# Some of the listed products of a graph layer, computed from 12-bit parts instead of in plain fp32

## The chip, the cores and the metric

The kernel runs on one core of one Trainium2 chip. The metric is the device time of one execution in microseconds; a comparison takes several runs of both kernels on the same chip. The profile is one further execution, recorded by the hardware profiler.

## The reference

Four layers work on a feature matrix x of 2708 x 512 and one sparse, symmetric-patterned adjacency matrix adj of 2708 x 2708. Each layer normalises its input, takes the relu, and adds its result to x. The layer that the change touches is layer 2:

```python
def _L2_gnn_ref(x, adj, W1, b1, W3, b3, Wf, bf):
    h = jax.nn.relu(adj @ (x @ W1) + b1)
    h = jax.nn.relu(adj @ (h @ W3) + b3)
    return jnp.tanh(h @ Wf + bf)
...
h = jnp.maximum(_layernorm(x, axis=-1), 0.0)
x = x + _L2_gnn_ref(h, adj, L2_gnn_W1, L2_gnn_b1, L2_gnn_W3, L2_gnn_b3, L2_gnn_Wf, L2_gnn_bf)
```

Everything is fp32. The adjacency matrix is dense in its first columns and rows and sparse in the rest: the chance of an entry falls with the square root of the row's and the column's number.

## The kernel before, in words

**Tiles.** The 2708 nodes are 22 row tiles of 128 (the last has 20). For a row tile m, the product adj @ g is made of two kinds of products of 128 x 128 by 128 x 512. The first six column tiles (DENSE = 6) are taken whole. Of the others, only the columns that hold an entry in this row tile are taken: layer 0 makes a list of them (`make_lists`, L290), and gathers and stores the adjacency columns that belong to the list (`listed`). `CHUNKS` (L38) tells how many products of 128 listed columns a row tile needs: none for tile 0, 10, 9 and 8 for tiles 1 to 3, 7 for tiles 4 to 7, then 6 and 5, and 2 for tile 21. That is 130 in all. Tile 0 has no list and takes all its column tiles (the `else` branch at L873); tile 21 has no dense part.

**Dense products in parts.** A dense piece of the adjacency (three tiles, 128 x 384) is loaded as `raw` and split into a 12-bit high part `hi`, the rest `lo`, and a sum `s` (L850 on ScalarE, L851 and L852 on VectorE). The features g are split likewise (`split_b`, L177). Three products in the type fp32r, hi x hi and lo x lo into the bank `main` and s x s into the bank `mixed`, take the place of one fp32 product (L863); the factors that `sum_banks` (L738) and the scales apply make the sum right. The buffers a_hi, a_lo and a_s have two copies each.

**Listed products.** `gather` (L810, issued at L814 on POOL) fetches for each product 128 rows of g from DRAM into one of eight buffers gg0 to gg7, which are used in turn over all row tiles. `load_listed` (L805) brings the adjacency columns as `ac`. Each listed product is one plain fp32 matmul into `mixed` (L866), in the order of the list, and is the last work of a row tile. `main` ends with the last dense product.

**The passes.** Layer 2 has two passes over the row tiles. The first (L956, order 0 to 9, 21, 10 to 20) aggregates g1 = h @ W1, adds the bias, takes relu, splits (`relu_parts`, L750) and multiplies by W3 (`project3`, L768: twelve fp32r products), and stores g2. While it works on tile 0 it also makes g1. It also writes a uint8 mask of the nonzero entries (L832) for layer 3. The second pass (L1125, order 0, 6 to 9, 21, 10 to 20, 1 to 5) aggregates g2, multiplies by Wf, applies tanh, adds to x, normalises, and multiplies by the weights of layer 3.

**Buffers of weights.** `wr` (1 MB, one buffer) is where a weight matrix lands before `split_w` splits it. In the first pass it holds Wf, which is split once tile 0 is done, and then the weights of layer 3, w_d, are loaded into it at once (L961). They are split into wb0 to wb2 in the second pass at tile 0 (L1129). Later `room` (L1005) hands out `wr` first as four places for gathers of layer 3, the first of which are issued with the last tile of the second pass.

**The order of the work.** The program is written as a sequence, and a scheduler fixes the order of each engine's instructions when the kernel is built: among those that its timing model takes to be ready, the one that comes first in the program goes first, and a buffer is given out when a previous user has released it. On the chip each engine runs its instructions in that fixed order; the DMA queues of SP and POOL too. So the dense products of row tile m+1 appear between the listed products of tile m and its projection. All of it lies in one function, of which the parts named here are the inner functions.

Of the kernel before, what the change touches and what calls it, by code (L numbers as in the profile page):

```python
# [8 lines left out]
FP = mybir.dt.float32  # L9
FR = mybir.dt.float32r  # L10
# [5 lines left out]
AF = mybir.ActivationFunctionType  # L16
ALU = mybir.AluOpType
# [4 lines left out]
P = 128  # L22
# [19 lines left out]
def kernel(  # L42
# [47 lines left out]
    def dense_of(m):  # L90

        return 0 if m == NT - 1 else DENSE
# [726 lines left out]
            )  # L819
        return gs  # L820

    def aggregate(m, parts, shifted, gd, marked):


        n = rows(m)
        whole, num = dense_of(m), CHUNKS[m]
        if marked:
            nz = ap.tile([P, NMARK, P], U8, name="nz", bufs=3)

            def mark(i, a):  # L830
                k, ts = a.shape[:2]
                nc.scalar.activation(nz[:k, i : i + ts, :n], a, AF.Sign)  # L832
        main = ps_a.tile([P, D], FP, name="agg") if dense_of(m) else None
        mixed = ps_a.tile([P, D], FP, name="aggs")
        chunks = []
        if num:
            ac = load_listed(m)
            chunks = [(ac[:, c, :], g) for c, g in enumerate(gather(m, gd))]
            if marked:
                mark(whole, ac)  # L840
        for ts in dense if dense_of(m) else []:
            gs = [parts(t) for t in ts]
            raw, k = load_piece(m, ts)
            hi, lo, s = (
                ap.tile([P, PIECE, P], FR, name=f"a_{part}") for part in ("hi", "lo", "s")
            )
            d = (slice(0, k), slice(0, len(ts)), slice(0, n))
            if marked:
                mark(ts[0], raw)
            nc.scalar.activation(hi[d], raw, AF.Copy, scale=UP)  # L850
            nc.vector.tensor_tensor(lo[d], raw, hi[d].bitcast(FP), ALU.subtract)  # L851
            nc.vector.scalar_tensor_tensor(  # L852
                s[d], lo[d].bitcast(FP), SHIFT, hi[d].bitcast(FP), op0=ALU.mult, op1=ALU.add
            )
            for i, t in enumerate(ts):
                ghi, glo, gs_ = gs[i]
                first, last = t == 0, t == DENSE - 1
                for acc, a, b, st, sp in (
                    (main, hi, ghi, first, False),
                    (main, lo, glo, False, last),  # L860
                    (mixed, s, gs_, first, False),
                ):
                    nc.tensor.matmul(acc[:n], a[:k, i, :n], b[:k], start=st, stop=sp)  # L863
        if chunks:
            for c, (a, g) in enumerate(chunks):
                nc.tensor.matmul(  # L866
                    mixed[:n],
                    a,
                    g,
                    start=(c == 0 and not dense_of(m)),  # L870
                    stop=(c == len(chunks) - 1),
                )
# [12 lines left out]
    def aggregated(m, parts, shifted, gd, bias, marked=False):  # L885
        n = rows(m)
        u = wp.tile([P, D], FP, name="u")
        main, mixed = aggregate(m, parts, shifted, gd, marked)
# [78 lines left out]
    bf = load_bias(bf_d, "bias0")  # L967
    bl = load_bias(b_d, "bias2")

# [659 lines left out]
```

## Time and profile before

| | us |
|---|---|
| median of 3 runs | 1551.56 |
| lowest and highest run | 1547.21, 1553.23 |
| the profiled execution | 1471.58 |
| its span, first to last instruction | 1469.7 |
| layers 0 and 1, and tile 0 of the first pass, in the span | 0 to about 641 |
| first pass of layer 2, tiles 1 to 20 | about 641 to 907 |
| seam: tile 0 of the second pass | about 907 to 945 |
| second pass of layer 2, other tiles | about 945 to 1262 |
| layer 3, the rest | about 1262 to 1470 |

The profiled execution has its own time, below the median of the unprofiled runs; durations are taken from it.

How to read the profile: PE is TensorE's matmul, PEld its weight load, DVE VectorE, ACT ScalarE, POOL GpSimd; SPq is the queue of SyncE, which issues most DMAs. A group's row gives the line, engine and operation, the tiles written and read, the count, then the busy time in us and the mean of one in ns, then the engine's idle time just before it and who ended it. A plain fp32 product has two MATMUL records, an fp32r product one. Matmuls are pipelined, so their cost is read from the distance of their starts and not from their length. In a stretch, each engine has its busy time and, in brackets, its instructions; then come the granted TensorE clock, the mean busy share of the 16 DMA engines, and the data rate. In the timeline the columns are start, length, engine, line, operation, tiles, count, and in square brackets the idle time before it and what ended it.

### The profile page before, as it was taken

The numbers are of one execution on the slowest core, as the hardware profiler recorded it, in microseconds if no ns is written. First come the engines' busy times: TensorE is split into PE (matmuls) and PEld (weight loads), VectorE is DVE, ScalarE is ACT, GpSimd is POOL, SyncE is SP. The second block draws the span as 40 slices with busy tenths as digits, with TensorE's granted clock in tenths as the row PEclk, the third lists the DMA queues.
The fourth block names the chain that finished last, engine by engine and source line by source line (L and its number), as shares of the span: only waits on it lengthen the run. The fifth ranks groups of instructions, "written<-read, shape, count | busy, mean of one in ns | idle before, by whom it ended". The sixth has DMA issues, their size and how long they took to land. (4 is left out here: it accounts for less than half of the span.)

```text
span 1469.7 us, 15561 instructions
## 1 busy us (share of the span) xinstructions
PE 1343.2 (91%) x4474; PEld 767.6 (52%) x4474; DVE 960.7 (65%) x1876; ACT 736.5 (50%) x1152; POOL 691.2 (47%) x690
## 2 busy tenths in 40 slices
PE   5489989999999869989999999899999999868997
PEld 2123334434334346755655666466677666656665
DVE  2566998998999679643433447365666665656675
ACT  5987864965521256432333335244554545454453
POOL 1162465876784341055554441333433445247763
PEclk9699989999999979999999999999999999889999
DMA  8896677788866398377786777856555666478884
GB/s 300 301 324 206 220 269 252 242 283 298 296 224 212 105 362 269 105 233 251 251 245 213 230 235 223 263 163 198 160 187 163 191 202 216 134 242 255 255 278 158
DMA packets 182415, 338.58 MB, mean 230 GB/s; under 512 B 25727, under 2 KB 94251, under 8 KB 178589
## 3 DMA queue, kind: packets, MB, share of 16 engines
q1 hardware_dynamic: 134929, 188.00, 38.1%
q0 software_dynamic: 47392, 149.51, 32.8%
q8 instruction: 37, 0.61, 0.2%
q14 instruction: 57, 0.47, 0.1%
HBM read 276.34 MB, written 61.09 MB: 230 GB/s over the span
## 5 line engine op out<-in xcount | busy, mean ns | idle before, releaser
L866 PE MATMUL aggs<-gg,ac 128*128 128x512 f32 (+1 forms) x520 | 232.7, 594 | 3.4 <-DMA gg<-g1d,idx_g 3.3
L814 POOL DMA_INDIRECT gg<-g2d,idx_g x130 | 131.2, 1009 | 217.6 <-PE aggs L866 168.6
L814 POOL DMA_INDIRECT gg<-g1d,idx_g x130 | 133.6, 1028 | 171.8 <-PE aggs L866 101.6
L478 POOL DMA_INDIRECT ac<-in_adj_t_dram,idx_a x130 | 144.8, 1114 | 79.8 <-issue 34.8
L660 PE MATMUL acc<-h,inc 128*128 128x512 f32 (+1 forms) x348 | 171.6, 626 | 6.4 <-ACT h L168 3.5
L496 POOL DMA_INDIRECT h<-h0d,idx_g x111 | 117.3, 1057 | 84.1 <-PE acc L660 58.8
L866 PEld LDWEIGHTS aggs<-gg,ac 128*128 128x128 f32 (+1 forms) x520 | 97.3, 188 | 110.6 <-issue 101.2
L850 ACT ACTIVATE a_hi<-raw 128x384 fp32r<-128x384 f32 x84 | 43.5, 520 | 158.0 <-issue 87.0
L863 PE MATMUL agg<-ghi,a_hi 128*128 128x512 f32 x252 | 115.0, 456 | 3.0 <-ACT a_hi L850 2.8
L660 PEld LDWEIGHTS acc<-h,inc 128*128 128x128 f32 (+1 forms) x348 | 63.8, 197 | 83.1 <-issue 65.6
L660 PE MATMUL acc<-h,incl 128*128 128x512 f32 (+1 forms) x222 | 104.3, 608 | 0.0
L863 PE MATMUL agg<-glo,a_lo 128*128 128x512 f32 x252 | 102.1, 405 | 1.3 <-ACT glo L189 1.3
L814 POOL DMA_INDIRECT gg<-hidr,idx_h x79 | 80.0, 1012 | 45.4 <-issue 13.1
L863 PE MATMUL aggs<-gs,a_s 128*128 128x512 f32 x252 | 100.2, 400 | 0.7 <-DVE a_s L852 0.6
L851 DVE TENSOR_TENSOR a_lo<-raw,a_hi 128x384 fp32r<-128x384 f32 x84 | 47.2, 562 | 76.4 <-ACT a_hi L850 49.9
L146 PE MATMUL yacc<-wvo,hT 128*128 128x512 f32 (+1 forms) x176 | 88.5, 642 | 4.2 <-ACT hT L175 4.2
L760 DVE SCALAR_TENSOR_TENSOR v_lo<-pt,v_hi 128x512 fp32r<-128x512 f32 (+1 forms) x88 | 56.5, 664 | 45.5 <-ACT v_hi L759 45.2
L741 DVE SCALAR_TENSOR_TENSOR u<-aggs,u 128x512 f32<-128x512 f32 x42 | 28.9, 687 | 75.4 <-PE aggs L866 73.9
L759 ACT ACTIVATE v_hi<-pt 128x512 fp32r<-128x512 f32 (+1 forms) x88 | 48.7, 579 | 44.1 <-PE pt L754 41.9
L660 PEld LDWEIGHTS acc<-h,incl 128*128 128x128 f32 (+1 forms) x222 | 40.7, 190 | 52.4 <-issue 50.8
L429 ACT ACTIVATE sgn<-ar 128x2708 bf16<-128x2708 f32 (+1 forms) x22 | 54.0, 2457 | 26.1 <-DMA ar<-in_adj_dram 22.5
L460 DVE FIND_INDEX8 at_top<-top,ar 128x8 uint32<-128x2708 f32 (+1 forms) x22 | 65.3, 2970 | 0.0
(268 smaller groups left out, 2897.1 us busy)
## 6 DMA issues: line engine op xcount, KB each, us to landing
ar<-in_adj_dram SPq DMA_DIRECT2D x27, 1354.0 KB
raw<-in_adj_t_dram SPq DMA_DIRECT2D x108, 192.0 KB
slot<-x SPq DMA_DIRECT2D x41, 256.0 KB
at<-in_adj_t_dram SPq DMA_DIRECT2D x27, 384.0 KB
ac<-lst SPq DMA_DIRECT2D x16, 384.0 KB
h<-in_x_dram SPq DMA_DIRECT2D x21, 256.0 KB
h0d<-h POOLq DMA_DIRECT2D x21, 256.0 KB, 5.7
xt<-in_x_dram SPq DMA_DIRECT2D x21, 256.0 KB
```

What stands on the lines that cost most here:

```text
L146: nc.tensor.matmul(acc[:n], hT[:, c, :n], w[:, c, :], start=(c == 0), stop=(c == NCD - 1))
L429: nc.scalar.activation(sgn[:n], ar[:n], AF.Sign, accum_out=sum_sgn[:n])
L460: nc.vector.max_index(at_top[:n], top[:n], ar[:n])
L478: nc.gpsimd.indirect_dma_start(out=ac[:, c, :n], out_offset=None, in_=adj_units, in_offset=bass.IndirectOffsetOnAxis(ap=idx_a[:, m, c0 + c ...
L496: nc.gpsimd.indirect_dma_start(out=g, out_offset=None, in_=h0d[:, :], in_offset=bass.IndirectOffsetOnAxis(ap=idx_g[:, m, c : c + 1], axis=0),)
L660: nc.tensor.matmul(acc[:n], a, g, start=(i == 0), stop=(i == len(pairs) - 1))
L759: nc.scalar.activation(hi[d], pt[d], AF.Relu, scale=UP)
L760: nc.vector.scalar_tensor_tensor(lo[d], pt[d], 0.0, hi[d].bitcast(FP), op0=ALU.max, op1=ALU.subtract)
L814: nc.gpsimd.indirect_dma_start(out=gs[c], out_offset=None, in_=gd[:, :], in_offset=bass.IndirectOffsetOnAxis(ap=index[:, m, c : c + 1], ax ...
L851: nc.vector.tensor_tensor(lo[d], raw, hi[d].bitcast(FP), ALU.subtract)
L863: nc.tensor.matmul(acc[:n], a[:k, i, :n], b[:k], start=st, stop=sp)
L866: nc.tensor.matmul(mixed[:n], a, g, start=(c == 0 and not dense_of(m)), stop=(c == len(chunks) - 1),)
```

## The change

In row tiles that have both a dense part and a list, the first `in_parts` listed products are computed from parts: three in the first pass, two in the second, and none in the last two row tiles of the second pass (tiles 4 and 5). Tiles 0 and 21 stay as they are. The other listed products stay plain fp32 and come first; the products in parts come last and end both banks. For them the adjacency columns in `ac` are split by ScalarE and VectorE like a dense piece, in one operation for all two or three, with the low part then rescaled on ScalarE. Each gathered row block is split by one ScalarE and two VectorE operations; its low part takes the place of the gathered rows, and its high part and sum go into one of two pairs of slots in the buffer `wr`. So w_d is no longer loaded early in the first pass but after it, and `wr` is used as slots again in the second pass once w_d has been split.

```diff
+    def split_a(raw, k, ts, n, scale_lo=None):
+        hi, lo, s = (
+            ap.tile([P, PIECE, P], FR, name=f"a_{part}") for part in ("hi", "lo", "s")
+        )
+        d = (slice(0, k), slice(0, ts), slice(0, n))
+        nc.scalar.activation(hi[d], raw, AF.Copy, scale=UP)
+        nc.vector.tensor_tensor(lo[d], raw, hi[d].bitcast(FP), ALU.subtract)
+        nc.vector.scalar_tensor_tensor(
+            s[d], lo[d].bitcast(FP), SHIFT, hi[d].bitcast(FP), op0=ALU.mult, op1=ALU.add
+        )
+        if scale_lo:
+            nc.scalar.activation(lo[d], lo[d].bitcast(FP), AF.Copy, scale=scale_lo)
+        return hi, lo, s
+
+    row_slot, part_rows = [0], [None]
+
+    def split_row(g):
+        i = row_slot[0] % 2 * 2
+        row_slot[0] += 1
+        hi, s = part_rows[0][:, i, :], part_rows[0][:, i + 1, :]
+        lo = g.bitcast(FR)
+        nc.scalar.activation(hi, g, AF.Copy, scale=UP * EPS12)
+        nc.vector.scalar_tensor_tensor(
+            lo, g, EPS12, hi.bitcast(FP), op0=ALU.mult, op1=ALU.subtract
+        )
+        nc.vector.scalar_tensor_tensor(
+            s, lo.bitcast(FP), SHIFT, hi.bitcast(FP), op0=ALU.mult, op1=ALU.add
+        )
+        return hi, lo, s
...
+        in_parts = in_parts if whole and num else 0
...
-                first, last = t == 0, t == DENSE - 1
+                first, last = t == 0, t == DENSE - 1 and not in_parts
...
-            for c, (a, g) in enumerate(chunks):
+            for c, (a, g) in list(enumerate(chunks))[in_parts:]:
                 nc.tensor.matmul(
                     mixed[:n],
                     a,
                     g,
-                    start=(c == 0 and not dense_of(m)),
-                    stop=(c == len(chunks) - 1),
+                    start=(c == 0 and not whole),
+                    stop=(c == num - 1 and not in_parts),
                 )
+            if in_parts:
+                hi, lo, s = split_a(ac[:, :in_parts], P, in_parts, n, -SHIFT)
+                for c in range(in_parts):
+                    ghi, glo, gs_ = split_row(chunks[c][1])
+                    last = c == in_parts - 1
+                    for acc, a, b, sp in (
+                        (main, hi, ghi, False),
+                        (main, lo, glo, last),
+                        (mixed, s, gs_, last),
+                    ):
+                        nc.tensor.matmul(acc[:n], a[:, c, :n], b, start=False, stop=sp)
...
     for m in order_m:
         n = rows(m)
-        parts = aggregated(m, first_parts, first_product, g1d, bias1, marked=True)
+        parts = aggregated(m, first_parts, first_product, g1d, bias1, True, 3)
         if m == 0:
             wf = split_w(wset, wr, "wa")
-            wr = load_w(wset, w_d, "wr")
+            part_rows[0] = wset.tile([P, NCD, D], FR, name="wr")
...
+    wr = load_w(wset, w_d, "wr")
     bf = load_bias(bf_d, "bias0")
...
     for m in order_2:
         n = rows(m)
-        parts = aggregated(m, second_parts, second_product, g2d, bias3)
+        in_parts = 0 if m in order_2[-2:] else 2
+        parts = aggregated(m, second_parts, second_product, g2d, bias3, False, in_parts)
         if m == 0:
             w = split_w(wsetb, wr, "wb")
+            part_rows[0] = wset.tile([P, NCD, D], FR, name="wr")
```

More of the change, by code (lines that the diff above doesn't have):

```diff
@@ L820, in gather, with aggregate @@
         return gs
-    def aggregate(m, parts, shifted, gd, marked):
+    def split_a(raw, k, ts, n, scale_lo=None):
[25 more added lines that the diff above has]
+        return hi, lo, s
+    def aggregate(m, parts, shifted, gd, marked, in_parts):
         n = rows(m)
         whole, num = dense_of(m), CHUNKS[m]
+        in_parts = in_parts if whole and num else 0
         if marked:
@@ L843, in aggregate @@
             raw, k = load_piece(m, ts)
[L844 to L847, printed above, removed]
             if marked:
                 mark(ts[0], raw)
[L850 to L854, printed above, removed]
+            hi, lo, s = split_a(raw, k, len(ts), n)
             for i, t in enumerate(ts):
                 ghi, glo, gs_ = gs[i]
-                first, last = t == 0, t == DENSE - 1
+                first, last = t == 0, t == DENSE - 1 and not in_parts
                 for acc, a, b, st, sp in (
@@ L883, in aggregate, with aggregated @@
         return main, mixed
-    def aggregated(m, parts, shifted, gd, bias, marked=False):
+    def aggregated(m, parts, shifted, gd, bias, marked, in_parts):
         n = rows(m)
         u = wp.tile([P, D], FP, name="u")
-        main, mixed = aggregate(m, parts, shifted, gd, marked)
+        main, mixed = aggregate(m, parts, shifted, gd, marked, in_parts)
         if dense_of(m):
```

## The prediction

> **What bounds the kernel now.** I read the busy shares first, then the costliest groups, then stretches of the span by stage, then one row tile of the first pass in order of time, then the gathers' time to landing. The page and its groups:
>
> ```profile
> PE 1343.2 (91%) x4474; PEld 767.6 (52%) x4474; DVE 960.7 (65%) x1876; ACT 736.5 (50%) x1152; POOL 691.2 (47%) x690
> ...
> L866 PE MATMUL aggs<-gg,ac 128*128 128x512 f32 (+1 forms) x520 | 232.7, 594 | 3.4 <-DMA gg<-g1d,idx_g 3.3
> L814 POOL DMA_INDIRECT gg<-g1d,idx_g x130 | 133.6, 1028 | 171.8 <-PE aggs L866 101.6
> ...
> L863 PE MATMUL agg<-ghi,a_hi 128*128 128x512 f32 x252 | 115.0, 456 | 3.0 <-ACT a_hi L850 2.8
> ```
>
> L866 is the listed products: 520 records for 260 products (130 a pass), so a product has two records. TensorE waits 3.4 us for all of them; the gathers' idle time (L814) is spent waiting for L866 to free a buffer. By stage (the two passes over the row tiles, and the seam between them):
>
> ```profile
> core 0: us, PE busy (x) PEld busy (x) DVE busy (x) ACT busy (x) POOL busy (x), PEclk, DMA share, GB/s
> 641.00:907.00 266.00, 262.88 (x924) 160.95 (x925) 112.44 (x187) 87.44 (x162) 126.82 (x126) 0.99 0.76 242
> 945.00:1262.00 317.00, 315.46 (x1206) 209.19 (x1205) 199.71 (x373) 156.85 (x234) 130.37 (x130) 1.00 0.60 185
> ...
> 907.00:945.00 38.00, 31.89 (x103) 19.07 (x102) 15.82 (x28) 10.09 (x19) 8.04 (x8) 0.91 0.79 259
> ```
>
> In both passes TensorE is busy 99% of the time at full clock; VectorE 42% and 63%, ScalarE 33% and 49%. Time taken off TensorE there is time off the kernel, as long as the others keep up. One tile of seven products in the first pass, in order of time:
>
> ```profile
> 703.36 0.39 PE L863 MATMUL aggs<-gs,a_s 128*128 128x512 f32 x1
> 703.59 6.17 PE L866 MATMUL aggs<-gg,ac 128*128 128x512 f32 x14
> ...
> 704.88 1.18 POOL L814 DMA_INDIRECT gg<-g1d,idx_g  x1 [3.15 <-PE aggs L866]
> 706.37 0.95 POOL L814 DMA_INDIRECT gg<-g1d,idx_g  x1 [0.30 <-PE aggs L866]
> 707.62 0.94 POOL L814 DMA_INDIRECT gg<-g1d,idx_g  x1 [0.30 <-issue]
> ...
> 709.82 0.39 PE L863 MATMUL agg<-glo,a_lo 128*128 128x512 f32 x1
> 709.87 0.69 DVE L741 SCALAR_TENSOR_TENSOR u<-aggs,u 128x512 f32<-128x512 f32 x1 [3.96 <-PE aggs L866]
> ...
> 711.43 0.63 PE L754 MATMUL pt<-ident,u 128*128 128x128 f32 x4
> ...
> 717.29 6.17 PE L866 MATMUL aggs<-gg,ac 128*128 128x512 f32 x14
> ```
>
> The period is 13.70 us (703.59 to 717.29). Fourteen records and one L863 lie between 703.59 and 709.82: (6.23 - 0.23) / 7 = 0.857 us a listed product. The dense part products (L863) start 0.23 us apart (703.36, 703.59), so three cost 0.69 us. While u (L741, L891) is summed, TensorE takes seven of the next tile's dense products: this is its cover. The gathers follow the freed buffers at 1.25 us each, the first 1.29 us after the block begins. Their landing, in the middle of the pass:
>
> ```profile
> DMA to landing us min/median/max: 3.5/4.5/5.8
> ```
>
> [...]
>
> **The change part by part.** *Products.* First pass: 20 tiles (all but 0 and 21) x 3 = 60; second: 20 less the last two = 18 tiles x 2 = 36. Each turns 0.857 into 0.69 us, 0.167 less: 60 x 0.167 = 10.0 and 36 x 0.167 = 6.0, together -16.0 us on TensorE, which sets the end of both passes.
>
> *Splits of the adjacency pieces.* Per tile two ScalarE and two VectorE operations. First pass at 384 columns: L850 0.52, L851 and L852 0.56 each. [...]
>
> *Splits of the gathered rows.* Each product adds L179's shape on ScalarE (0.62) and L183's and L186's on VectorE (0.69 + 0.68). So VectorE gets, per tile, 1.12 + 3 x 1.37 = 5.2 us in the first pass (20 x: 105) and 0.85 + 2 x 1.37 = 3.6 in the second (18 x: 65). Its share becomes (112 + 105) / 256 = 85% and (200 + 65) / 311 = 85%. ScalarE gets 1.04 + 1.86 = 2.9 (58 in all) and 0.84 + 1.24 = 2.1 (37): (87 + 58) / 256 = 57% and (157 + 37) / 311 = 62%. All of it lies beside TensorE's 256 and 311 us; I take 0. If that cover fails at the end of each tile, the cost is the slower rival's.
>
> *The end of a tile.* main now stops with the last split product, so the sum starts with ScalarE's 0.58 (L740) after it, which was long done before. Also c2, the third split row, waits for the pair of hi and s that c0 used: hi 0.62, lo 0.69, s 0.68, about 2.4 with handovers, against c1's 0.69 of products. What is late next is the sum of u; the cover is the next tile's 18 dense products, 18 x 0.23 = 4.1 us. I take 0. What is queued behind the waiting row split on VectorE and ScalarE is the next tile's a_lo and a_hi, for which TensorE would wait. Bounds: 0 to 2 us a tile; not below zero, since nothing leaves this chain.
>
> *Gather buffers.* There are eight, taken in turn, and the first of a tile's buffers is the one that POOL needs first, but it is now used last. In a tile of seven, four plain products (3.4) and hi and lo of c0 (0.46) come before it is free: with the 0.43 that the trace shows after a product's end, the first gather goes at 4.3 instead of 1.3. One buffer was spare, six follow: the last goes at 4.3 + 5 x 1.25 = 10.6 and lands at 15.1. It is needed at (13.70 - 0.50) + 3 x 0.857 = 15.8: on time by 0.7 us at the median landing, late by 0.6 at the longest. Tiles of six and five have two and three spare buffers, so are safe. Wider ones are not. Tile 2 (nine, behind ten) starts at buffer 2, tile 1's c2, free at about 6.0 + 2.0 + 0.4 = 8.4; its nine gathers land by 8.4 + 8 x 1.25 + 4.5 = 22.9, needed at about 15.5 + 5 x 0.857 = 19.8. Three late; as the scheduler can put the split products (2.1) first, 1 to 3, I take 2. Tile 3 likewise: 6.7 + 8.75 + 4.5 = 20.0 against 18.4, late by 1.6, I take 1; tile 4, whose first buffer isn't spare either, 0.5. Tile 1 itself: TensorE already waits 3.3 us for the first row (at 641.27), which must now be split (2 us) or passed over: +1, bounds -2 (see the moved load) to +3. Second pass: more work lies between two blocks (period 16.0), only tile 1 (ten) and tile 2 refill from themselves: +1, bounds 0 to 4.
>
> *The moved load.* The 1 MB load of wr (L152) leaves 634.6, where the queues are at 90 to 100% and the first gather is late, for the end of the pass, when c2 of the last tile frees the buffer, about 908 on SP. There bias loads, x2, raw and listed pieces queue behind it, and POOL's gathers share the engines. From 910 to 920 the DMA share is 0.31 and 0.79, so 4.5 us of all engines are free for about 3 us of data at the 340 to 390 GB/s of 920 to 935. But right after, TensorE waits 5.4 us for raw pieces: I take +1, bounds -1 to +4. The weights' own splits have until 952.
>
> Sum: -16.0 + 3.5 (tiles 2 to 4) + 1 + 1 + 1 = -9.5 us. The profiled execution takes 1471.6 (span 1469.7), so 1462; the median of the three runs, 1551.6, is 80 us above it, which the profile doesn't explain, so I carry the difference over: 1551.6 - 9.5 = 1542.
>
> **The rivals.**
> *Full gain.* The scheduler orders around the late gathers and the freed 1 MB helps tile 1: -16, 1536. For it: TensorE had almost no waits before. Against: the buffer count above.
> *Late gathers throughout.* The tiles of seven slip too (0.6 and more, twelve wide tiles over both passes)[...]: 12 x 0.7 = 8 more, 1550, no change.
> *VectorE sets the second pass.* 85% in an order fixed in advance, with tanh and the normalisation between: the second pass gains nothing (6 back) and loses 0.1 us a tile: 1550.
> *The end of a tile is exposed* (slower). The split piece takes one of the two a_ buffers, so the next tile's second half of dense products (9 x 0.23 = 2.1) can't be split before the last listed product. Chain from c0's products to the transposes: 0.62 + 0.69 + 0.68 + 0.58 + 0.69 + 0.69 plus seven handovers of 0.15 = 5.0 us; cover without that half is 0.69 + 2.1 = 2.8. Up to 2.2 are bare; half of it on 20 tiles is +22: 1542 + 22 = 1564. It decides from 9.5 / 20 = 0.5 us a tile. Against it: the two parts of the chain overlap with the dense products' own splits (1.9 us).
> That the change does nothing is excluded: the products exist in every tile.
>
> **How the numbers follow.** Forecast 46% (of it 6% within the bound), full gain 14%, late gathers 12%, VectorE 8%, exposed end 20%. 0.5%, about what a measurement of this kernel can tell from no change, is 7.8 us. Faster: 0.40 + 0.14 = 0.54; same: 0.06 + 0.12 + 0.08 = 0.26; slower 0.20. Half the exposed cases end below 1564, so the range is 1532 to 1564, with some 15% outside. The likeliest side's own range is 1532 to 1543.
>
> **What would show it.** Right: L866 falls from 520 to 328 records; split products 0.23 us apart; TensorE still 98 to 99% busy in both passes; periods of seven near 13.2 and second-pass periods of six near 15.7; short waits of L866 for gg in tiles 1 to 4 only; VectorE near 85%. Wrong: a TensorE wait of over 0.5 us in each tile, on a row split, on a_hi or on u; waits for gg in tiles of seven or six; or a seam longer by more than 4 us.

## The result, and the profile after

The changed kernel takes 1655.91 us (median of 3 runs, 1643.7 to 1657.72) against 1551.56: 1.0656 times the time before, 95% interval 1.057 to 1.0742. It is slower, and outside the range that was given. Its profiled execution has a span of 1654.1 us. The page (busy row, then groups):

```profile
PE 1403.1 (85%) x4570; PEld 814.6 (49%) x4570; DVE 1105.8 (67%) x2144; ACT 822.1 (50%) x1324; POOL 703.0 (42%) x690
...
L814 POOL DMA_INDIRECT gg<-g1d,idx_g x130 | 137.3, 1056 | 227.1 <-PE aggs L893 132.5
L893 PE MATMUL aggs<-gg,ac 128*128 128x512 f32 (+1 forms) x328 | 164.6, 626 | 35.8 <-DMA gg<-g1d,idx_g 25.0
```

L866 is L893 now: 328 records, as forecast. But TensorE waits 35.8 us for gathered rows in front of them, where it waited 3.4. The first pass, the second pass and the seam between them:

```profile
core 0: us, PE busy (x) PEld busy (x) DVE busy (x) ACT busy (x) POOL busy (x), PEclk, DMA share, GB/s
688.00:1016.00 328.00, 285.50 (x999) 185.30 (x998) 203.59 (x347) 139.28 (x259) 128.68 (x124) 0.92 0.63 197
1045.00:1405.00 360.00, 323.82 (x1224) 218.58 (x1223) 244.21 (x464) 180.01 (x294) 135.08 (x127) 0.96 0.52 160
1016.00:1045.00 29.00, 22.74 (x59) 11.38 (x58) 13.54 (x23) 9.00 (x16) 8.84 (x8) 0.89 0.93 307
```

The profile of the kernel before that the prediction read is 80 us under that kernel's median, and the two traces differ in layers 0 and 1 too, which the change doesn't touch. So I took one more profiled execution of the kernel before (e1), whose span is 1536.8. Its two passes:

```profile
680.00:962.00 282.00, 273.40 (x958) 168.15 (x959) 117.54 (x195) 91.87 (x170) 126.59 (x126) 0.99 0.73 233
990.00:1313.00 323.00, 320.44 (x1222) 212.18 (x1221) 202.26 (x378) 158.57 (x236) 131.18 (x130) 1.00 0.60 184
```

The first pass is 46 us longer (328 against 282): 34 us more in which TensorE is idle (42.5 against 8.6), and 12 us more in which it is busy, at a clock of 0.92 in place of 0.99. The second is 37 us longer in these stretches, 34 of them idle. The stretches were cut by eye and the changed kernel's end earlier in the work, the second by about one row tile; between the same points of the work (the table below) the passes are 54 and 59 us longer. The loss lies in the two passes, in TensorE's waits and in the lower clock beside them (0.92 for 0.99 and 0.96 for 1.00).

One tile of the changed kernel's first pass, in order of time (weight loads, VectorE and most products left out):

```profile
801.15 0.84 ACT L867 ACTIVATE nz<-ac 128x768 uint8<-128x768 f32 x1 [2.25 <-DMA ac<-lst]
...
801.44 0.95 POOL L814 DMA_INDIRECT gg<-g1d,idx_g  x1 [0.30 <-issue]
...
801.75 0.60 PE L754 MATMUL pt<-ident,u 128*128 128x128 f32 x4
801.90 0.51 ACT L828 ACTIVATE a_hi<-ac 128x384 fp32r<-128x384 f32 x1
...
802.88 0.40 PE L890 MATMUL aggs<-gs,a_s 128*128 128x512 f32 x1
...
803.74 0.63 ACT L846 ACTIVATE wr<-gg 128x512 fp32r<-128x512 f32 x1 [1.33 <-DMA gg<-g1d,idx_g]
804.28 0.51 ACT L867 ACTIVATE nz<-raw 128x384 uint8<-128x384 f32 x1
...
804.69 0.58 ACT L759 ACTIVATE v_hi<-pt 128x512 fp32r<-128x512 f32 x1
...
805.94 1.66 PE L893 MATMUL aggs<-gg,ac 128*128 128x512 f32 x2 [2.67 <-DMA gg<-g1d,idx_g]
...
806.61 2.70 PE L779 MATMUL main<-wb,v_hi 128*128 128x512 f32 x4
...
809.10 1.42 PE L779 MATMUL main<-wb,v_lo 128*128 128x512 f32 x4
```

The transposes (L754) are done at about 802.3, and v_hi (L759), which the projection (L779) needs, could follow at once. Ahead of it in ScalarE's fixed order stand four things of the next tile: the mark of its listed columns (L867, it waits 2.25 us for the load of `ac`), the high part of the columns of three products (L828), a row split (L846, waits 1.33 us for a gathered row) and a mark of a dense piece. The first two are through at 802.4; in this tile it is the row split's wait that holds v_hi back, until 805.27. Ahead of the projection in TensorE's order stands a plain listed product of the next tile (L893); its row was issued at 801.44 and is there at 805.94, 4.5 us later and 0.67 us after v_hi, so here that is the wait that ends last. TensorE idles 2.67 us, and then two groups of four projection products take 2.70 us (with the end of the plain product in it) and 1.42 us, where the kernel before needs about 1.1. There, in e1, the order is the other way round:

```profile
772.61 0.60 ACT L759 ACTIVATE v_hi<-pt 128x512 fp32r<-128x512 f32 x1
...
773.34 1.12 PE L779 MATMUL main<-wb,v_hi 128*128 128x512 f32 x4
...
774.56 0.85 ACT L832 ACTIVATE nz<-ac 128x768 uint8<-128x768 f32 x1 [1.34 <-DMA ac<-lst]
```

From row tile 3 on, the mark of `ac` follows v_hi of the tile before in every row tile of the kernel before, and stands ahead of it in every one of the changed kernel but tile 11. TensorE's order changed too: in the changed kernel's first pass a plain listed product of the next tile stands between the transposes and the projection in 12 row tiles, and TensorE waits for its row 9 times, 17.4 us in all; in the kernel before this is so in none. TensorE's two largest waits in the changed kernel's first pass, 688 to 1016 (engine, line, the one waited for, us in total, times, longest; the first also holds 7.6 us in tiles 1 and 2, at the listed products' own place):

```profile
PE aggs L893 <- DMA gg<-g1d,idx_g: 25.0, 12, 4.2
PE main L779 <- ACT v_hi L759: 11.3, 6, 4.1
```

The second pass has no marks. A tile of it in the changed kernel, in order of time:

```profile
1116.99 1.03 PE L754 MATMUL pt<-ident,u 128*128 128x128 f32 x8
...
1118.34 0.39 PE L890 MATMUL aggs<-gs,a_s 128*128 128x512 f32 x1
...
1122.26 1.29 ACT L846 ACTIVATE wr<-gg 128x512 fp32r<-128x512 f32 x2 [5.22 <-DMA gg<-g2d,idx_g]
...
1123.45 1.07 ACT L759 ACTIVATE v_hi<-pt 128x512 fp32r<-128x512 f32 x2
...
1124.09 2.07 PE L779 MATMUL main<-wb,v_hi 128*128 128x512 f32 x4 [5.36 <-ACT v_hi L759]
...
1125.96 1.05 PE L779 MATMUL main<-wb,v_lo 128*128 128x512 f32 x2
```

Two row splits wait 5.22 us for gathered rows, two v_hi are queued behind them, and TensorE waits 5.36 us for the first of them; then it works at half speed for some 3 us (the granted clock is 0.50 from 1123.84 to 1127.25).

### The profile page after: what moved, and what is told of

It is laid out like the page before. It is cut to its first block, busy times and chain, and to the rows that moved or that the text cites. A ratio compares the mean times of both kernels' runs of the same rounds, so it can differ in the third digit from the quotient of the medians.

```text
span 1654.1 us, 16430 instructions
## 1 busy us (share of the span) xinstructions
PE 1403.1 (85%) x4570; PEld 814.6 (49%) x4570; DVE 1105.8 (67%) x2144; ACT 822.1 (50%) x1324; POOL 703.0 (42%) x690
## 5 line engine op out<-in xcount | busy, mean ns | idle before, releaser
L893 PE MATMUL aggs<-gg,ac 128*128 128x512 f32 (+1 forms) x328 | 164.6, 626 | 35.8 <-DMA gg<-g1d,idx_g 25.0
L660 PE MATMUL acc<-h,inc 128*128 128x512 f32 (+1 forms) x348 | 172.8, 630 | 3.7 <-ACT h L168 1.2
L146 PE MATMUL yacc<-wvo,hT 128*128 128x512 f32 (+1 forms) x176 | 100.1, 714 | 25.3 <-issue 13.3
L847 DVE SCALAR_TENSOR_TENSOR gg<-gg,wr 128x512 fp32r<-128x512 f32 x96 | 65.4, 687 | 72.5 <-ACT wr L846 54.7
L846 ACT ACTIVATE wr<-gg 128x512 fp32r<-128x512 f32 x96 | 59.6, 626 | 101.2 <-PE agg L910 28.4
L890 PE MATMUL agg<-ghi,a_hi 128*128 128x512 f32 x252 | 103.2, 410 | 5.5 <-ACT a_hi L828 4.2
L893 PEld LDWEIGHTS aggs<-gg,ac 128*128 128x128 f32 (+1 forms) x328 | 61.7, 196 | 91.3 <-issue 40.3
L660 PE MATMUL acc<-h,incl 128*128 128x512 f32 (+1 forms) x222 | 104.7, 611 | 0.0
L660 PEld LDWEIGHTS acc<-h,inc 128*128 128x128 f32 (+1 forms) x348 | 64.6, 199 | 80.6 <-issue 70.7
L779 PE MATMUL main<-wb,v_hi 128*128 128x512 f32 (+1 forms) x176 | 67.1, 511 | 24.0 <-ACT v_hi L759 22.5
L850 DVE SCALAR_TENSOR_TENSOR wr<-gg,wr 128x512 fp32r<-128x512 f32 x96 | 65.4, 684 | 15.8 <-PE aggs L910 14.5
L146 PEld LDWEIGHTS yacc<-wvo,hT 128*128 128x128 f32 (+1 forms) x176 | 36.8, 221 | 75.1 <-issue 57.8
L830 DVE SCALAR_TENSOR_TENSOR a_s<-a_lo,a_hi 128x384 fp32r<-128x384 f32 (+1 forms) x122 | 64.9, 534 | 9.9 <-PE aggs L910 2.7
L759 ACT ACTIVATE v_hi<-pt 128x512 fp32r<-128x512 f32 (+1 forms) x88 | 48.4, 575 | 44.4 <-PE pt L754 32.0
```

Source lines behind the costliest of these rows:

```text
L146: nc.tensor.matmul(acc[:n], hT[:, c, :n], w[:, c, :], start=(c == 0), stop=(c == NCD - 1))
L660: nc.tensor.matmul(acc[:n], a, g, start=(i == 0), stop=(i == len(pairs) - 1))
L779: nc.tensor.matmul(acc[:n], a[:, c, :n], b[:, c, :], start=first and c == 0, stop=last and c == NCD - 1,)
L830: nc.vector.scalar_tensor_tensor(s[d], lo[d].bitcast(FP), SHIFT, hi[d].bitcast(FP), op0=ALU.mult, op1=ALU.add)
L847: nc.vector.scalar_tensor_tensor(lo, g, EPS12, hi.bitcast(FP), op0=ALU.mult, op1=ALU.subtract)
L850: nc.vector.scalar_tensor_tensor(s, lo.bitcast(FP), SHIFT, hi.bitcast(FP), op0=ALU.mult, op1=ALU.add)
```

## The experiments

**Theories.** Q: the row splits and the re-ordered plain products wait for gathered rows and stand, in an order fixed at build time, ahead of the previous tile's v_hi and projection. M, formed after e8: in the first pass the marks do the same, waiting for the loads of the adjacency. W: the splits' work on ScalarE and VectorE is itself the bound. B: the split of the listed adjacency holds one of the two a_ buffers. L: late gather buffers in tiles of seven and more. (That the order is kept on the chip is seen where both programs are still the same: the first 1593 matmul records of TensorE, 564 instructions of ScalarE, 1052 of VectorE, 562 of GpSimd and 279 DMA issues of SyncE come in the same sequence in the profiles of before and after, though the second is 43 us behind at the first product in parts.)

**How they are read.** Ratios are to the kernel before on the same chip. The runs were made in batches, each on another chip: e1 to e4 on chip 0, e5 to e7 on chip 1, e8 to e10 on chip 6, e11 to e14 on chip 5, e15 to e17 on chip 8, e18 on chip 7; for the result and the first profile no chip is recorded. The stages come from each profiled execution: first pass from the end of layer 1's products (L660) to the last store of g2, second pass from there to the last store of the tiles' results `hid`. Where the kernel before takes about 1480 us, layers 0 and 1 take 499 to 509 us, and where it takes about 1550, 538 to 551, whatever the kernel; each line is to be compared with the kernel before of its own group, not with a line of the other.

| kernel | ratio, 95% interval | first pass, us | second pass, us |
|---|---|---|---|
| *before takes about 1540 to 1550* | | | |
| before (e1) | | 425.0 | 395.0 |
| the change | 1.0656, 1.057 to 1.0742 | 479.5 | 454.1 |
| e2 rotated, plain | 1.0069, 1.0038 to 1.01 | 424.9 | 393.8 |
| e3 last in parts | 1.0814, 1.0717 to 1.0911 | 474.7 | 472.8 |
| e4 first pass only | 1.0297, 1.0194 to 1.04 | 467.5 | 396.9 |
| e11 products, marks behind | 1.0111, 1.0051 to 1.0171 | 438.7 | 401.1 |
| e12 marks behind | 1.0539, 1.0493 to 1.0586 | 448.9 | 458.3 |
| e13 marks, rows behind last v_hi | 1.119, 1.1141 to 1.1239 | 433.3 | 584.2 |
| e14 before, marks behind | 1.003, 1.0007 to 1.0052 | 425.1 | 396.8 |
| e18 marks, rows behind first v_hi | 1.0228, 1.0186 to 1.0269 | 425.4 | 425.4 |
| *before takes about 1480* | | | |
| before (the profile shown first) | | 414.7 | 391.3 |
| e5 ordered | 1.1835, 1.1808 to 1.1861 | 474.2 | 614.4 |
| e6 resident rows | 1.0388, 1.036 to 1.0417 | 447.9 | 415.4 |
| e7 products alone | 1.0217, 1.018 to 1.0254 | 447.7 | 394.7 |
| e8 clean products | 1.0247, 1.022 to 1.0274 | 460.7 | 393.8 |
| e9 rows only | 1.054, 1.0492 to 1.0589 | 460.3 | 431.5 |
| e10 adjacency only | 1.0361, 1.0341 to 1.0382 | not used | not used |
| e15 six only | 1.0276, 1.0243 to 1.0309 | 417.7 | 431.6 |
| e16 seven, second pass | 1.0184, 1.0151 to 1.0218 | 418.4 | 420.0 |
| e17 six, rows behind | 1.0239, 1.0211 to 1.0268 | 413.6 | 428.7 |

e16's first pass is the kernel before and measures 418.4 against 414.7, so a stage of that order is good to some 4 us. The change's order repeats less well: e4's first pass has that order on every engine and measures 467.5 against 479.5, 12 us apart. (e10's profiled execution was 19 us above its median; its stages are not used.)

### e1: the kernel before once more

> The kernel before once more, for its stages on the same chip as the others. The profile shown of it took 1471.6 us, 80 less than its median, and its layers 0 and 1 (537 us to the first product in parts) are 43 us shorter than in the profile of the changed kernel, though the change doesn't touch them. If that is a difference between chips or executions, this profile should have layers 0 and 1 near 580 and a span near 1550; the two passes should stay near 266 and 317. If the change lengthens the early layers, this profile stays near 537.

No edit. 1538.6 us. It gives the stages to compare with, and shows that the 80 us between the first profile and the median are not in the change.

### e2: the change's order of use alone

```diff
+            turn = (3 if marked else 2) if whole and num <= 8 else 0
+            if not marked and m in order_2[-2:]:
+                turn = 0
-            for c, (a, g) in enumerate(chunks):
+            for c, (a, g) in enumerate(chunks[turn:] + chunks[:turn]):
```

> The kernel before with one edit: in row tiles with a dense part and at most eight listed products, the plain products are taken in the order c3, c4, ..., c0, c1, c2 (first pass; from c2 in the second). No parts, no splits, no moved load. Theory of late gathers (buffers c0 to c2 are freed last, though the next tile's first plain row goes into one of them): TensorE gets waits for gathered rows in many tiles, 10 to 40 us slower. Theory of the splits (the added ScalarE and VectorE work is what TensorE waits for): no change, 1552.

The kernel before, with the first three (two) rows of a tile used last, as in the change, but plain (row tiles 1 and 2 stay as they are). 0.7% slower, both passes unchanged within the 4 us. Using the first rows last is at most a small part of the 6.6%.

### e3: the last products in parts, in the natural order

```diff
-            for c, (a, g) in list(enumerate(chunks))[in_parts:]:
+            for c, (a, g) in list(enumerate(chunks))[: num - in_parts]:
...
-                hi, lo, s = split_a(ac[:, :in_parts], P, in_parts, n, -SHIFT)
+                hi, lo, s = split_a(ac[:, num - in_parts :], P, in_parts, n, -SHIFT)
```

> The changed kernel with the last three (two) listed products in parts instead of the first, so that buffers are freed in the order in which they are filled again; the split work is the same. Theory of late gathers: the waits for gathered rows (36 us in the changed kernel) go, and the half clock after them; 1540 to 1580. Theory of the splits: the last rows land last and are split last, so it stays at 1640 or above.

Slower than the change itself (1.0814). The waits moved, they did not go: TensorE waits 29.1 us in the first pass for v_hi (14 times; 44.3 us and 21 times in both passes), hardly for rows (2.8 us), and ScalarE's row splits wait 36.1 us for gathered rows. That the buffers come free in the wrong order was my first theory; it fell here. The same waits on another engine led to theory Q.

### e4: the first pass only

```diff
-        in_parts = 0 if m in order_2[-2:] else 2
+        in_parts = 0
```

> The changed kernel with three products in parts in the first pass and none in the second. The first pass grew from 266 to 330 us between the profiles and the second from 317 to 360. If the passes add up, this keeps about 60 of the 104 us: 1610. If the moved load or what comes after is the cost, it stays near 1655.

First pass +42, second +2. The passes' losses are separate, and the moved load of w_d, which this kernel keeps, costs nothing that can be seen.

### e5: all of it queued behind the previous tile

```diff
+        with late("act"):
             nc.scalar.activation(hi, g, AF.Copy, scale=UP * EPS12)
...
+        with late("dve"):
...
+                with late("pe"):
                     nc.tensor.matmul(
...
```

(`late` queues the instruction in its engine's order behind v_hi, v_s and the last projection product of the tile before; nothing waits for anything new.)

> The changed kernel with one thing added: in TensorE's, ScalarE's and VectorE's fixed order, what needs a tile's gathered rows (plain listed products, row splits) is queued behind the projection, v_hi and v_s of the tile before. Same work, same buffers. Theory Q (gathered rows that land late stand in the queues ahead of the previous tile's v_hi and projection): most of the loss goes, 1530 to 1590, and the waits of the projection for v_hi and of plain products for gg ahead of it fall from about 60 us to under 20. Theory W (the work of the splits on ScalarE and VectorE is itself the bound): the order does nothing, 1630 or more.

Far worse (1.1835), and neither theory expected that. In the second pass TensorE waits 111.1 us, 22 times up to 5.5 us, for the normalised u (L168): between a tile's two projections lie tanh and the normalisation, and the listed products that filled this gap now stood behind it. The first pass gained nothing (+60), so Q as I had put it was not enough there: TensorE still waits 24.4 us for v_hi. What still stands ahead of v_hi in e5's trace, in nearly every row tile, is the marks and the split of the listed adjacency; the plain products and the row splits all stand behind.

### e6 and e7: the splits without gathered rows, and the products alone

e6 splits a resident part of g instead of the gathered row (other data in the rows in parts); e7 leaves all splits out and takes resident parts:

```diff
-        lo = g.bitcast(FR)
-        nc.scalar.activation(hi, g, AF.Copy, scale=UP * EPS12)
+        _, lo, g = g
+        nc.scalar.activation(hi, g.bitcast(FP), AF.Copy, scale=UP * EPS12)
...
-                    ghi, glo, gs_ = split_row(chunks[c][1])
+                    ghi, glo, gs_ = split_row(gs[i])
```

```diff
-                hi, lo, s = split_a(ac[:, :in_parts], P, in_parts, n, -SHIFT)
...
-                    ghi, glo, gs_ = split_row(chunks[c][1])
+                    ghi, glo, gs_ = gs[i]
...
-                        nc.tensor.matmul(acc[:n], a[:, c, :n], b, start=False, stop=sp)
+                        nc.tensor.matmul(acc[:n], a[:k, i, :n], b[:k], start=False, stop=sp)
```

> The changed kernel, but each row split reads a part of g that is resident instead of the gathered row (so the listed rows in parts hold other data); the same number of ScalarE, VectorE and TensorE instructions and all gathers are kept, the split waits for no gather. Theory Q: the waits of ScalarE for gathers go, some plain products still wait ahead of the projection: 1540 to 1600. Theory W: 1630 or more, as nothing of the work has gone.

> The changed kernel without the splits: the three products of each listed tile taken in parts read parts that are resident (other data), no adjacency split, no row split; gathers are kept. It gives TensorE's gain alone. By the 0.167 us a product of the prediction, 96 products give 16 us: 1535 if nothing waits; theories Q and W both expect 1530 to 1550. If it stays over 1580, the loss is in the products or in the gathers' buffers and not in the splits or what they wait for.

(The expectations of e5 to e7 are in us for a kernel before of about 1550; in this group it took 1478.57, so the ratios are what to compare.) e6 is at 1.0388 against the change's 1.0656: all the work is there; gone are the splits' wait for gathered rows and, as nothing reads these rows any more, the products' hold on their buffers, and with them some 2.7 of 6.6%. So the work alone is not the cause. But e7, which has no split at all, still loses 33 us in the first pass, where both theories had expected no loss.

### e8, e9, e10: products, row splits and adjacency split one by one

e8 takes the adjacency's parts from resident tiles too, so that no a_ buffer is held; e9 adds the true row splits, e10 the true adjacency split (what is not true is other data):

```diff
-                hi, lo, s = split_a(ac[:, :in_parts], P, in_parts, n, -SHIFT)
+                hi, lo, s = (x.rearrange("p (c m) -> p c m", m=P) for x in gs[i])
...
-                    ghi, glo, gs_ = split_row(chunks[c][1])
+                    ghi, glo, gs_ = gs[i]
```

> As e7 (three products for each listed tile taken in parts, no splits), but their operands come from parts that are resident for the whole pass, so that no a_ buffer is held through them. Theory B (a_hi, a_lo and a_s have two buffers, the parts of the listed adjacency take or hold one until the products are through, and the next tile's second dense piece comes late, with its marks and loads, so that TensorE's gaps at the end of a tile are not filled): the 33 us that e7 lost in the first pass go, ratio to before 0.985 to 1.00. If the ratio stays at 1.015 or over, e7's loss is in the order or in the gathers and not in the held buffer.

> The changed kernel with real row splits on gathered rows, but the listed adjacency's parts replaced by resident ones (no adjacency split, no a_ buffer taken). Theory Q (row splits that wait for gathered rows stand in the fixed order ahead of other work): ratio 1.03 to 1.06. Theory B alone: at or below 1.01.

> The changed kernel with the real adjacency split (it takes an a_ buffer), but the rows' parts replaced by resident ones (no row split). Theory B: like e7, ratio 1.02 to 1.035, most of it in the first pass. Theory Q alone: at or below 1.005.

B fell: e8 holds no buffer and loses 46 us in the first pass. Its second pass is that of the kernel before, within the 4 us, and the true row splits add 38 us there (e9, 431.5 against 393.8), so the second pass's loss comes with the row splits. e10 is 1.1% above e8: the adjacency split costs something too. The waits of e8 in its first pass (654 to 960), engine and line, the one waited for, us in total, times, longest:

```profile
...
ACT nz L867 <- DMA raw<-in_adj_t_dram: 52.3, 15, 6.0
ACT nz L867 <- DMA ac<-lst: 49.6, 18, 4.4
...
PE main L779 <- ACT v_hi L759: 30.4, 16, 3.3
```

and those of the kernel before (e1, 680 to 965):

```profile
...
ACT nz L832 <- DMA ac<-lst: 22.0, 14, 2.6
ACT nz L832 <- DMA raw<-in_adj_t_dram: 21.5, 15, 3.5
```

ScalarE's marks wait for loads in both. In e8 the projection waits for v_hi behind them, 16 times: theory M. (No plain product stands ahead of a projection in e8's first pass, so this is not TensorE's order.)

### e11, e12, e14: the marks behind v_hi

```diff
+    def behind_v_hi():
+        return tc.issue_after(v_hi_last[-1].ins) if v_hi_last else ExitStack()
...
-        nc.scalar.activation(hi[d], pt[d], AF.Relu, scale=UP)
+        v_hi_last.append(nc.scalar.activation(hi[d], pt[d], AF.Relu, scale=UP))
...
-                nc.scalar.activation(nz[:k, i : i + ts, :n], a, AF.Sign)
+                with behind_v_hi():
+                    nc.scalar.activation(nz[:k, i : i + ts, :n], a, AF.Sign)
```

(`issue_after` fixes the order on ScalarE only; the other engines' order is again what the scheduler makes of it. e11 is this in e8, e12 in the change, e14 in the kernel before.)

> e8 (three products for each listed tile in parts, all operands resident, no splits) with one thing added: in ScalarE's fixed order the marks (sign of the loaded adjacency) of a tile are queued behind v_hi of the tile before. Theory M (in the first pass the marks, which wait for the adjacency's loads, stand ahead of v_hi in the changed kernels and behind it in the kernel before): the 46 us that e8 lost in the first pass go, ratio to before 0.985 to 1.00. If M is wrong: as e8, 1.02 to 1.03.

> The whole change, with the marks queued behind v_hi of the tile before in ScalarE's order. Theory M: of the 54 us that the first pass lost some 30 to 45 go, what row splits and gathers cost stays; the second pass is not touched: ratio 1.035 to 1.05. If the marks are not what the first pass waits for: 1.06 or more.

> The kernel before with the marks queued behind v_hi in the same way. It has them there by itself in nearly every tile, so theory M expects no change beyond 0.5%: 0.995 to 1.005. A larger gain or loss would mean that the added order does something else too.

M holds: e11 loses 14 us in the first pass where e8 lost 46, and e14 shows that the same order brings the kernel before nothing (0.3% slower). e12's first pass is 31 us shorter than the change's in the profiles; the whole times say less, 1.0539 for 1.0656, about 18 us. And e12 is not the marks alone: in the new order a plain product stands ahead of the projection in 3 row tiles of the first pass, without a wait, where the change has 12. TensorE's largest waits there, 690 to 1000 (those for rows are in tiles 1 and 2):

```profile
PE main L784 <- ACT v_hi L764: 13.8, 7, 2.6
PE aggs L899 <- DMA gg<-g1d,idx_g: 11.3, 4, 4.9
```

So e12 can't tell the place of the marks from the place of the plain products. e5 can: its plain products stand behind the projection and its marks ahead of v_hi, and its first pass gained nothing. e11 also shows the size of the saving: in tiles 11 to 14 (six listed products) the stores of g2 are 12.1 us apart, in e14 12.9. e11's whole is 1.0111, over the 1.00 that was expected: its tiles 1 and 2 take 54.2 us together against e14's 42.2.

### e13 and e18: the row splits behind v_hi too

```diff
+        with behind_v_hi():
             nc.scalar.activation(hi, g, AF.Copy, scale=UP * EPS12)
```

e13 is e12 with this; in e18 `v_hi_last` takes only the first v_hi of a tile, that of the listed sums:

```diff
-        v_hi_last.append(nc.scalar.activation(hi[d], pt[d], AF.Relu, scale=UP))
+        v_hi = nc.scalar.activation(hi[d], pt[d], AF.Relu, scale=UP)
+        if first:
+            v_hi_last.append(v_hi)
```

> As e12, and the row splits of a tile too are queued behind the last v_hi of the tile before, in ScalarE's order alone (TensorE's and VectorE's are left to themselves, other than in e5). Theory Q, that row splits waiting for gathered rows hold v_hi up: 1.00 to 1.035. If in the second pass late row splits leave nothing to fill TensorE's gaps, as in e5: 1.06 or more.

> The whole change, nothing left out, with the marks and the row splits of a tile queued in ScalarE's order behind the first v_hi of the tile before (the one of the listed sums), where e13 queued them behind its last v_hi, which in the second pass is that of the second projection. Theory Q for both passes: the first pass stays as in e13 (about 8 us over the kernel before) and the second loses its waits of 4 to 5 us for v_hi: 10 to 30 us over the kernel before instead of 59 (the change) or 126 (e13); ratio 1.00 to 1.025. If what holds the second pass up is not the row splits' place: 1.04 or more.

In e13 the first pass comes down another 16 us, to 8 over the kernel before, where e5, with the marks ahead of v_hi, is 60 over. But the second pass rises to 584: as in e5, what could fill the gap between the projections is too late, and TensorE waits 55.0 us there for the normalised u and 41.7 us for gathered rows. e18 leaves nothing of the change out, adds no buffer and prescribes nothing but ScalarE's order (in its first pass, too, a plain product stands ahead of a projection in 3 row tiles only): ratio 1.0228 for 1.0656. Its passes:

```profile
684.00:970.00 286.00, 269.20 (x1024) 177.54 (x1022) 210.09 (x355) 143.17 (x274) 134.73 (x127) 0.99 0.76 237
985.00:1340.00 355.00, 326.00 (x1245) 216.50 (x1246) 252.45 (x477) 185.17 (x303) 123.89 (x122) 0.99 0.55 170
```

The clock is 0.99 again in both, and the first pass is level with the kernel before (425.4 against 425.0); tiles of six take 12.3 us for e14's 12.9. VectorE works as much as in the change (210 us for 204 in the first pass), so its work was not what held the first pass up. The second pass keeps 30 us of 59, spread evenly: row tiles 11 to 18 take 17.3 to 18.0 us each there, in e1 15.8 to 17.5. TensorE's largest wait in its stretch (engine, line, the one waited for, us, times, longest):

```profile
PE aggs L902 <- DMA gg<-g2d,idx_g: 16.4, 23, 2.1
```

One place of it, in order of time:

```profile
1213.57 0.94 POOL L821 DMA_INDIRECT gg<-g2d,idx_g  x1 [9.19 <-PE agg L919]
...
1217.20 1.12 PE L902 MATMUL aggs<-gg,ac 128*128 128x512 f32 x2 [0.77 <-DMA gg<-g2d,idx_g]
```

POOL waits 9.19 us for a product in parts (L919) to free its buffer, and the rows behind come a little late for the plain products (L902).

### e15, e16, e17: tiles of six and of seven apart

```diff
-        in_parts = in_parts if whole and num else 0
+        in_parts = in_parts if whole and 0 < num <= 6 else 0
```

(e15, on e12; e17 queues the first pass's row splits behind v_hi as well. e16, on the change, has `num > 6 and not marked`.)

> As e12 (marks behind v_hi), and only row tiles with at most six listed products take any of them in parts, in both passes; tiles with seven to ten stay plain. Theory L (with eight gather buffers, a tile of seven or more leaves the next one a buffer that a product in parts, taken last, frees only at the end of the tile, and the later gathers queue behind that one): the second pass loses under 15 us instead of e12's 60, the whole is 0.99 to 1.015. If row splits cost as much in tiles of five and six: second pass 30 us or more over, whole 1.02 to 1.04.

> The complement, in the second pass alone: the first pass is the kernel before, and in the second pass only the five row tiles with seven to ten listed products take two of them in parts (10 products in all). Theory L: these five tiles lose about 5 us each, also through the tile behind them: 20 to 35 us, ratio 1.013 to 1.023. If the loss goes with the number of products in parts: a quarter of 59 us at most, ratio 1.00 to 1.01.

> As e15, and in the first pass the row splits too are queued behind v_hi of the tile before (e13 gained 16 us there by it; the second pass is left as in e15). Theories M, Q and L together: first pass 0 to 10 us under the kernel before, 3 to 10 us under e15's; whole 0.985 to 1.01.

L fell as the only cause: tiles of five and six alone lose 40 us in the second pass (e15), where L expected under 15. The ten products of the other five tiles lose 29 (e16), as L expected. Both kinds pay; e16's tiles pay more for each product. e17's first pass is level with the kernel before (413.6 against 414.7). No version tried beats the kernel before.

## Why the prediction was wrong, step by step

- **The saving of a product** (0.857 to 0.69 us) was right: products in parts start 0.23 us apart in the changed trace, and tiles of six shrink from 12.9 us (e14) to 12.3 once the order is mended (e18), 0.6 for the 0.5 forecast.
- **"All of it lies beside TensorE's 256 and 311 us; I take 0"** is the step that failed. I compared shares of busy time. VectorE's work was even less than forecast (145 us more on the page, 1105.8 against 960.7, for 170). The splits of the adjacency at 256 columns, which the trace of before lacks (the forecast's sums have 0.85 us a tile for VectorE and 0.84 for ScalarE), take 0.84 (L829 0.418, L830 0.420) and 0.82 (L828 0.409, L834 0.408) in the changed trace. But the new ScalarE instructions start by waiting for gathered rows, and the whole fixed order moved, so that instructions that wait for loads stand ahead of v_hi and of the projection. Both together cost, by e18 against the change, 54 us in the first pass and 29 in the second, in single profiles; by the whole times 4.3%, some 66 us of the 104.
- **What is queued behind the wait** was named wrongly: "the next tile's a_lo and a_hi". It is v_hi of the tile before, and TensorE's projection behind that.
- **The rest of the order** was taken as that of the kernel before. It is not: with part of the products in parts the marks moved ahead of v_hi in nearly every tile. From e8 to e11 that alone is 32 us of the first pass. No line of the diff touches the marks, and the prediction doesn't mention them. Why the scheduler moved them is not shown; e8 shows that the products alone bring it about.
- **When a gathered row is needed** was reckoned inside the next listed block, so that tiles of seven, six and five came out safe. In the changed kernel a plain product of the next tile often stands ahead of the projection, far earlier, and TensorE waits there 9 times in the first pass, 17.4 us. Waits for gg in tiles of six and seven were one of the prediction's signs of being wrong. The order in which the buffers come free was not the trouble there (e2, e3).
- **The clock** had no term. In the changed trace's tile of the second pass, after the wait of 5.36 us, four products take 2.07 us at a granted clock of 0.50 (from 1124.09); four later ones take 1.07 at 1.00 (from 1127.95). For shorter waits see the last section. Of the 46 us of the first pass's stretch, 12 are more busy time; e18, with the same products at a clock of 0.99, is busy 269.2 us there where the change, at 0.92, is busy 285.5.
- **The moved load, the seam and tiles 1 and 2**: the load is right (e4, +2 with an error of 4). The seam, from the last store of g2 to the first of `hid`, takes 48.1 us in the changed kernel and 43.6 in e1: 4.5 more, about the 4 us that the prediction allowed. Tiles 1 and 2 cost 5 us more in e18 than in e14 (47.0 against 42.2), near the 3 that were given.
- **The rivals.** The exposed end of a tile had the right side and place, but its mechanism, the held a_ buffer, is not what e8 shows, and its price (22 us) was a fifth of the loss. (Of its handovers of 0.15 us, the one from the last sum of u, L891, to the transposes, L754, is 0.145 in the trace of before, the median of 19 in the first pass; that from the first sum, L741, to the last is 0.034.)
- **Open:** 30 us of the second pass in e18. Of the 29 us that TensorE idles there, 16.4 are waits for gathered rows. Against that, e6, whose splits wait for no row, has a second pass 22 us over e8's, so part is the splits' own work or the a_ buffer. More gather or a_ buffers, which could separate them, weren't tried.

## What to carry to other kernels

Before costing new work on an idle engine at nothing, ask what each new instruction waits for and what stands behind it in that engine's queue: here a 0.6 us split that waits 5 us for a row held up a whole projection. Where a tool fixes the order at build time, any change can move instructions that it doesn't touch, so read the order of both kernels around the critical hand-over before believing a share of busy time. A wait of TensorE should be priced with the clock behind it: here the waits of 2.67 and 5.36 us shown above were each followed by 3.41 us at a granted clock of 0.50.

## What was not expected of the hardware

- Layers 0 and 1, the same code in all kernels, take 499 to 509 us in the batches on chips 1, 6 and 8 and 538 to 551 on chips 0, 5 and 7, and the kernel before takes about 1480 or 1550 us with it. Each batch had one chip, so whether it is the chip or something else about the batch stays open. One profile of before beside a median from elsewhere can be 80 us off before anything is changed.
- Some waits of under 3 us were followed by half the clock. The one of 2.67 us in the first-pass tile above ends at 805.94; in the 3.41 us up to 806.40 TensorE is busy for 0.74, and the granted clock is 0.50 for the next 3.41 us. Waits of 2.05 and 2.16 us in the same pass (from 821.17 and 960.26) are followed by 0.50 too, from 823.46 and 963.41; after those of 1.72 and 2.84 us at 985.49 and 1408.55 it stays at 1.00 for the next 16 us at least. What decides is not shown. The rows around the wait of 2.67 us:

```profile
core 0: us, PE busy (x) PEld busy (x) DVE busy (x) ACT busy (x) POOL busy (x), PEclk, DMA share, GB/s
802.99:806.40 3.41, 0.74 (x3) 0.30 (x2) 2.87 (x6) 2.35 (x5) 0.00 (x0) 1.00 0.55 202
806.40:809.81 3.41, 3.41 (x8) 2.29 (x7) 1.82 (x4) 0.00 (x0) 1.27 (x1) 0.50 0.24 57
```
